# Transposing the next graph's x1 ahead of a graph's last product, in one stretch of a two-layer graph network

## The chip, the core and the metric

The kernel runs on one core of a Trainium2 chip. The core has five engines that run side by side, each with its own queue of instructions: TensorE (PE, matrix products; its weight loads are listed as PEld), VectorE (DVE), ScalarE (ACT), GpSimd (POOL) and SyncE (SP, which here only issues transfers). TensorE writes its results into banks of PSUM; everything else lives in SBUF or in DRAM. The metric is the device time of one execution in microseconds (us), the median of several.

## The reference

64 graphs of 256 nodes with 256 features go through two layers. Layer 0 is a normalised graph convolution, layer 1 a block made of a convolution along the nodes, an attention product and a gated unit. Cut to what is computed:

```python
# layer 0
deg = adj.sum(-1); d = where(deg != 0, deg, 1) ** -0.5
a_plus = d[:, :, None] * adj * d[:, None, :] + max(alpha, 1e-10) * eye(N)
x = layernorm(x + (a_plus @ x) @ W.T + b)              # called x1 in the kernel
# layer 1
h = relu(bn1(conv1(x.T)))                              # 1x1 convolution
x_conv = relu(bn2(conv2(h)) + x.T).T                   # 17 taps along the nodes
s = x @ w_se.T + b_se
A = exp(-dist(s, s)) * adj
x_nmp = A @ relu(x @ w_msg.T + b_msg)
x = layernorm(x + gru(concat(x_conv, x_nmp), x))       # gates r, z and candidate n
```

## The kernel before

The 17-tap convolution is done in the frequency domain. Sixteen graphs (Q) make a group, and there are four groups (NQ). For each graph `layer1` puts a small Fourier transform of h into a tile V; when a group is complete, `products` multiplies V with the transformed taps (matrices u, streamed from DRAM by SP), one step of 12 after another, and the inverse transform (`real_transform`, `complex_begin`, `complex_end`), which is vector work on VectorE, writes the convolution's result to DRAM. `gates` then runs the gated unit of each graph.

The work is written as generators that are woven into each other. `layer0` has three pieces, `layer1` seven. `graphs` runs `layer1` of graph g piece by piece, with pieces of `layer0(g + 2)` after pieces 1, 4 and 5, and of another stage (`others`) after pieces 0 and 5. The pieces of `layer1` are: (0) four transposes of x1 into a PSUM bank p_x1T and a copy on ScalarE into the first half of the tile xn (lines 413 to 420); (1) p_conv1, which reads that half, with VectorE adding the bias into h (line 431) and a relu on ScalarE (line 432); (2) p_msg; (3) p_dft, the Fourier transform of h (line 463), copied into V; (4) p_rows, with the copies dist_l on ScalarE and dist_r on VectorE; (5) p_dist (line 487), two Exp on ScalarE, and the product with the adjacency on VectorE (aT, line 489); (6) p_nmp (line 494), the graph's last product, copied into the second half of xn (line 498), which is then stored to DRAM (line 499). `layer0(g)` ends with p_out (line 398), VectorE's line 403 and a layernorm, whose power runs on GpSimd (line 314) and whose last step on ScalarE (line 324); that makes x1, two of which exist at a time. Its first piece transposes the adjacency (p_adjT, line 367, copied by line 368) and scales x (line 380).

The first sixteen graphs run while the weights are set up. Then the main loop goes over the groups q. While the products of group q run, the graphs of group q + 1 begin: the first AHEAD of them (12 for q = 0, 6 later) write their transforms into a second tile V2. With q = 0 no gates are due yet, so `others` is empty: three pieces of the graphs 16 to 27 are run after each of the 12 steps of products, and the rest is run by `paced`, which hands out pieces of `complex_end` on VectorE behind marked instructions of the graphs, 1.2 pieces for each mark. Then four copies on ScalarE (line 1031) bring V2 into V, the memory of V2 is given to the tiles of the gates, and the last four graphs (28 to 31) run with the first gates of group 0 as `others`. The gates' first pieces load xc_g (line 742) and the inputs (lines 746, 748), add x1 into xc_g by a transfer that GpSimd issues (line 753), transpose it (p_xcT, line 764), and form sums on GpSimd (lines 775 to 780).

Inside each engine the order isn't the order in which the program is written: a planner goes over all instructions, takes the written order as their priority, and gives each engine the instruction that its own estimate has ready. `issue_after` ties an instruction to a place behind another one. PSUM banks of `layer0` and `layer1` come from one ring of four (`bank`), in the order in which they are asked for.

Of the kernel before, what the change touches and what calls it, by code (L numbers as in the profile page):

```python
# [9 lines left out]
F32 = mybir.dt.float32  # L10
# [4 lines left out]
P = 128  # L15
# [11 lines left out]
def kernel(  # L27
# [27 lines left out]
    nc = tc.nc  # L55
    B, N, D = x.shape
# [4 lines left out]
    DCH = D // P  # L61
# [14 lines left out]
    work = ctx.enter_context(tc.tile_pool(name="work", bufs=2))  # L76
# [3 lines left out]
    def bank(name):  # L80
        return ps.tile([P, 512], F32, tag="bank", name=name)
# [7 lines left out]
    def mark(op):  # L89
        marks.append(op.ins)  # L90
# [238 lines left out]
    xc_d = [dram.tile([Q, N, D], F32, name=f"xc_d{q}") for q in range(NQ)]  # L329
    x1_d = [dram.tile([Q, N, D], F32, name=f"x1_d{q}") for q in range(NQ)]  # L330
    xn_d = [dram.tile([P, 2 * DCH, N], F32, name=f"xn_d{g}") for g in range(B)]
    ADJT, X1, X_SCALED, DIAGONAL = {}, {}, {}, {}


# [73 lines left out]
        nc.scalar.dma_start(x1_d[g // Q][g % Q].rearrange("(c p) d -> p c d", p=P), x1)  # L408
        yield

    def layer1(g, V, place):

        x1, adjT = X1.pop(g), ADJT.pop(g)
        xn = work.tile([P, 2 * DCH, N], F32, name="xn")
        x1T = xn[:, :DCH]
        p = bank("p_x1T").rearrange("p (k n) -> p k n", k=DCH)
        for k in range(DCH):
            for c in range(NCH):
                nc.tensor.transpose(p[:, k, c * P : (c + 1) * P], x1[:, c, k * P : (k + 1) * P], ident)
        nc.scalar.copy(x1T, p)  # L420

        yield

        h = work.tile([P, NCH, D + NSE], F32, name="h", bufs=1)
        for c in range(NCH):
            p = bank("p_conv1")[:, : D + NSE]
            for k in range(DCH):
                nc.tensor.matmul(  # L428
                    p, x1T[:, k, c * P : (c + 1) * P], wc1[:, k, :], start=k == 0, stop=k == DCH - 1
                )  # L430
            mark(nc.vector.tensor_tensor(h[:, c, :], p, bc1, op=ALU.add))
        nc.scalar.activation(h[:, :, :D], h[:, :, :D], AF.Relu)  # L432

        s3 = h[:, :, D:]
        cols = scols.rearrange("p c (q r) -> p c q r", r=32)
        nc.vector.tensor_copy(cols[:, :, :, :NSE], s3.unsqueeze(2).to_broadcast([P, NCH, 4, NSE]))
        sq3 = small.tile([P, NCH, NSE], F32, name="sq3")
        nc.vector.scalar_tensor_tensor(sq3, s3, -1.0, s3, op0=ALU.mult, op1=ALU.mult)
        nsq = small.tile([P, NCH], F32, name="nsq")
        nc.vector.tensor_reduce(nsq, sq3, AX.X, ALU.add)  # L440
        nc.vector.tensor_scalar(
            cols[:, :, 2:4, NSE], nsq.unsqueeze(2).to_broadcast([P, NCH, 2]), 0.5, None, op0=ALU.mult
        )
        yield
        msg = work.tile([P, NCH, D], F32, name="msg", bufs=1)
        p = bank("p_msg").rearrange("p (c d) -> p c d", c=NCH)
        for c in range(NCH):
            for k in range(DCH):
                nc.tensor.matmul(  # L449
                    p[:, c, :], x1T[:, k, c * P : (c + 1) * P], wmsg[:, k, :], start=k == 0, stop=k == DCH - 1  # L450
                )
        mark(nc.vector.tensor_tensor(msg, p, bmsg_t.unsqueeze(1).to_broadcast([P, NCH, D]), op=ALU.add))  # L452
        nc.scalar.activation(msg, msg, AF.Relu)
        yield


        mid = GT // 2
        for k in range(DCH):
            p = bank("p_dft")

            for c, t0, t1 in ((0, 0, mid + 1), (1, mid - 1, GT)):
                first = t0 + 1 - c * mid
                nc.tensor.matmul(  # L463
                    p[:, t0 * FL : t1 * FL], h[:, c, k * P : (k + 1) * P],
                    fwd[:, first : first + t1 - t0, :].rearrange("p t f -> p (t f)"),
                    start=c == 0, stop=True, skip_group_check=c == 1,
                )
            nc.scalar.copy(
                V[:, :, k, place * GT : (place + 1) * GT],
                p[:, : GT * FL].rearrange("p (t f) -> p f t", f=FL),  # L470
            )

        yield
        p = bank("p_rows")
        for c in range(NCH):
            nc.tensor.transpose(p[:, c * P : (c + 1) * P], scols[:, c, :], ident)
        dl = work.tile([64, N], F32, name="dist_l", bufs=1)
        nc.scalar.copy(dl, p[0:64, :N])
        dr = work.tile([64, N], F32, name="dist_r", bufs=1)
        nc.vector.tensor_copy(dr, p[64:P, :N])  # L480
        yield

        aT = work.tile([P, NCH, 2, P], F32, name="aT", bufs=1)
        for c in range(NCH):
            rows = slice(32 * c, 32 * c + 32)
            p = bank("p_dist")[:, :N]
            nc.tensor.matmul(p, dl[rows, c * P : (c + 1) * P], dr[rows, :], start=True, stop=True)
            nc.scalar.activation(aT[:, c].rearrange("p n q -> p (n q)"), p, AF.Exp, bias=nsq[:, c : c + 1], scale=2.0)  # L488
        mark(nc.vector.tensor_mul(aT, aT, adjT[:, :, 0:3:2, :]))  # L489
        yield  # L490
        p = bank("p_nmp").rearrange("p (k n) -> p k n", k=DCH)
        for k in range(DCH):
            for mc in range(NCH):
                nc.tensor.matmul(  # L494
                    p[:, k, :], msg[:, mc, k * P : (k + 1) * P], aT[:, mc].rearrange("p n q -> p (n q)"),
                    start=mc == 0, stop=mc == NCH - 1,
                )
        nc.scalar.copy(xn[:, DCH:], p)
        nc.scalar.dma_start(xn_d[g], xn)
        yield  # L500
# [5 lines left out]
    V, M = VM.rearrange("p f (k q) -> p f k q", k=DCH), VM  # L506
# [369 lines left out]
    def take(stage, n):  # L876

        for _ in range(n):
            if next(stage, "end") == "end":
                return  # L880
            yield
# [6 lines left out]
    def run(stage):  # L888
        for _ in stage:
            pass  # L890
# [18 lines left out]
    def graphs(first, part, V, others):  # L909


        for i in part:
            load(first + i + 3)
            given = {"layer0": layer0(first + i + 2) if first + i + 2 < B else iter(()), "other": others[i]}
            for piece, _ in enumerate(layer1(first + i, V, i)):
                yield
                for name in PLACES[piece]:
                    if next(given[name], "end") != "end":
                        yield
            yield from given["other"]  # L920
# [68 lines left out]
    def nothing():  # L989
        return iter(())  # L990
# [4 lines left out]
    scope, AHEAD, V2 = open_ahead(12)  # L995
    late = nothing()
    for q in range(NQ):
        first = (q + 1) * Q
        more = q + 1 < NQ
        end = complex_end(q)  # L1000
        if more:
            if q:
                others = [take(late, 3 if i % 3 == 0 else 2) for i in range(AHEAD)]
            else:
                others = [nothing() for _ in range(AHEAD)]
            begin = graphs(first, range(AHEAD), V2, others)
        sums(0)
        real = real_transform()
        for step in range(STEPS):
            if step < 4:  # L1010
                run(products(step))
            else:
                run(merge(products(step), take(real, 1)))
                run(complex_begin(step))
            if q:
                run(take(late, (0, 1, 1, 1, 1, 1, 2, 1, 2, 1, 2, 1)[step] if more else step % 2))
            else:
                run(take(begin, 3))
        run(real)
        if not q:  # L1020
            run(paced(begin, end, RATES[q]))
        elif more:
            run(paced(chain(merge(take(late, 20), take(begin, 6), 3), begin), end, RATES[q]))
        else:
            run(paced(late, end, RATES[q]))
            run(end)
        if more:
            run(late)
            run(end)
            for f in range(0, FL, 12):  # L1030
                nc.scalar.copy(V[:, f : f + 12, :, : AHEAD * GT], V2[:, f : f + 12])
            if q == 0:
                scope.close()
                gate = ctx.enter_context(tc.tile_pool(name="gate", bufs=2))
            early = gates(q, range(EARLY))
            others = [take(early, 5 if q == 0 else 2) for _ in range(Q)]
            run(graphs(first, range(AHEAD, Q), V, others))
            run(early)
            if q == 0:
                scope, AHEAD, V2 = open_ahead(6)  # L1040
                ctx.enter_context(scope)
            late = gates(q, range(EARLY, Q))
        else:
            run(gates(q, range(Q)))
# [53 lines left out]
```

## Time and profile before

| what | value |
|---|---|
| median of 3 runs | 2172.98 us (2172.46 to 2173.61) |
| the profiled execution | 2174.33 us, of which the span shown by the profile is 2172.5 us |
| instructions | 29034 |
| mean granted clock of TensorE | 0.989 of full speed |
| the stretch of graphs 16 to 27 | about 275 to 521 us from the span's start |
| of it, among the products of group 0 | 288 to 395 us |
| of it, with complex_end alone | 395 to 521 us |
| V2-to-V copies (line 1031) | 4 of about 2.1 us, at 515.17, 520.07 and two from 524.95 us |
| graphs 28 to 31 with the first gates | about 530 to 647 us |

The profile is of one execution. A timeline line gives the start in us, the busy time in us, the engine, the line of the kernel, the operation, what it writes and reads, and how many instructions were merged; in brackets stands how long the engine stood idle before it, and what ended that. A line of waits gives the engine and line that waited, for whom, the total in us, how often, and the longest. A matrix product in f32 shows as two records for each matmul of the program, so four matmuls are listed as 8; transposes are one record each. Busy times of consecutive products overlap a little, because the end of a product is modelled: the distance between the starts is the better measure of what one takes.

### The profile page before, as it was taken

The numbers are of one execution on the slowest core, as the hardware profiler recorded it, in microseconds if no ns is written. First come the engines' busy times: TensorE is split into PE (matmuls) and PEld (weight loads), VectorE is DVE, ScalarE is ACT, GpSimd is POOL, SyncE is SP. The second block draws the span as 40 slices with busy tenths as digits, with TensorE's granted clock in tenths as the row PEclk, the third lists the DMA queues.
The fourth block names the chain that finished last, engine by engine and source line by source line (L and its number), as shares of the span: only waits on it lengthen the run. The fifth ranks groups of instructions, "written<-read, shape, count | busy, mean of one in ns | idle before, by whom it ended". The sixth has DMA issues, their size and how long they took to land. (4 is left out here: it accounts for less than half of the span.)

```text
span 2172.5 us, 29034 instructions
## 1 busy us (share of the span) xinstructions
PE 2064.0 (95%) x9805; PEld 1748.4 (80%) x9805; DVE 1550.7 (71%) x3691; ACT 834.3 (38%) x1847; POOL 664.2 (31%) x640
## 2 busy tenths in 40 slices
PE   7999999887999999999999999899999998999998
PEld 5788788776788887788888888778888887788887
DVE  5555568785568798775556989775555889977776
ACT  4566643455331122455453122346543112222222
POOL 2444310211431233313222133323231123444442
PEclk9999999999999999999999999999999999999999
DMA  4765656434337644344335754334334844444442
GB/s 129 223 194 178 216 185 207 154 125 141 97 112 226 194 123 122 107 119 121 104 99 175 208 163 116 110 117 132 101 97 124 250 117 122 120 123 107 112 101 60
DMA packets 251182, 305.65 MB, mean 141 GB/s; under 512 B 18174, under 2 KB 229714, under 8 KB 251034
## 3 DMA queue, kind: packets, MB, share of 16 engines
q1 hardware_dynamic: 183530, 200.46, 30.4%
q10 hardware_dynamic: 44480, 67.39, 8.7%
q0 software_dynamic: 23024, 35.95, 8.6%
q8 instruction: 78, 1.28, 0.2%
q14 instruction: 70, 0.57, 0.1%
HBM read 200.62 MB, written 103.06 MB: 140 GB/s over the span
## 5 line engine op out<-in xcount | busy, mean ns | idle before, releaser
L833 PE MATMUL p_n<-wn,inputs 128*128 128x256 f32 x1536 | 355.9, 385 | 11.0 <-DVE first L809 10.6
L796 PE MATMUL p_rz<-wrz,sums 128*128 128x256 f32 x1536 | 350.9, 382 | 3.2 <-POOL sums L775 2.3
L833 PEld LDWEIGHTS p_n<-wn,inputs 128*128 128x128 f32 x1536 | 289.1, 192 | 58.1 <-DVE first L809 14.5
L796 PEld LDWEIGHTS p_rz<-wrz,sums 128*128 128x128 f32 x1536 | 290.7, 191 | 48.2 <-issue 5.9
L796 PE MATMUL p_rz<-wrz,inputs 128*128 128x256 f32 x1152 | 271.7, 379 | 0.4 <-ACT inputs L766 0.4
L314 POOL TENSOR_TENSOR ln_rs<-ln_rs,neg_half 128x2 f32<-128x2 f32 x129 | 101.2, 784 | 527.9 <-DVE ln_rs L313 417.4
L796 PEld LDWEIGHTS p_rz<-wrz,inputs 128*128 128x128 f32 x1152 | 217.5, 190 | 30.3 <-ACT inputs L766 1.0
L845 ACT ACTIVATE nn<-gn 128x256 f32<-128x256 f32 x128 | 53.2, 416 | 333.2 <-DVE gn L842 333.0
L518 PE MATMUL p_k<-u,VM 128*128 128x256 f32 x736 | 175.3, 380 | 4.1 <-DMA u<-ud 3.3
L775 POOL TENSOR_TENSOR sums<-inputs 128x384 f32<-128x384 f32 x64 | 67.8, 1059 | 335.1 <-ACT inputs L766 327.0
L358 POOL TENSOR_TENSOR dis<-deg,neg_half 128x2 f32<-128x2 f32 x64 | 46.5, 726 | 402.6 <-DVE deg L356 395.6
L324 ACT ACTIVATE x_g<-x_g,ln_mr,ln_rs 128x256 f32<-128x256 f32 x128 | 70.0, 593 | 245.6 <-DVE ln_mr L322 242.0
L518 PEld LDWEIGHTS p_k<-u,VM 128*128 128x128 f32 x736 | 138.1, 190 | 25.7 <-DMA u<-ud 3.4
L428 PE MATMUL p_conv<-wc,xn 128*128 128x259 f32 x512 | 128.8, 394 | 19.6 <-ACT xn L420 18.5
L388 PE MATMUL p_hT<-adjT,x 128*128 128x256 f32 x512 | 126.6, 390 | 9.5 <-DVE msg L452 4.9
L381 POOL TENSOR_TENSOR x_t<-x_t,b_t 128x512 f32<-128x512 f32 x64 | 86.4, 1350 | 146.7 <-ACT x L380 89.3
L463 PE MATMUL p_dft<-fwd,h 128*128 128x240 f32 x512 | 117.8, 373 | 13.9 <-ACT h L432 13.0
L428 PEld LDWEIGHTS p_conv<-wc,xn 128*128 128x128 f32 x512 | 97.1, 194 | 39.8 <-ACT xn L420 24.1
L489 DVE TENSOR_TENSOR aT<-aT,adjT 128x512 f32<-128x512 f32 x64 | 44.3, 692 | 115.3 <-ACT aT L488 115.3
L398 PE MATMUL p_out<-w,hT 128*128 128x256 f32 x512 | 123.9, 385 | 2.5 <-ACT hT L393 2.1
L449 PE MATMUL p_msg<-wmsg,xn 128*128 128x256 f32 x512 | 121.3, 379 | 0.0
L494 PE MATMUL p_nmp<-aT,msg 128*128 128x256 f32 x512 | 121.1, 379 | 0.2 <-DVE aT L489 0.2
(154 smaller groups left out, 3894.9 us busy)
## 6 DMA issues: line engine op xcount, KB each, us to landing
u<-ud SPq DMA_DIRECT2D x284, 256.0 KB
xn_d<-xn ACTq DMA_DIRECT2D x64, 512.0 KB
inputs<-xn_d SPq DMA_DIRECT2D x64, 512.0 KB
ud<-u_set POOLq DMA_DIRECT2D x39, 480.0 KB, 6.2
adj_t<-in_adj_dram SPq DMA_DIRECT2D x64, 256.0 KB
x_t<-in_x_dram SPq DMA_DIRECT2D x64, 256.0 KB
x_d<-x ACTq DMA_DIRECT2D x64, 256.0 KB
xc_d<-VM SPq DMA_DIRECT2D x64, 256.0 KB
```

What stands on the lines that cost most here:

```text
L314: nc.gpsimd.tensor_tensor(rs[:, : len(chunks)], rs[:, : len(chunks)], neg_half[:, : len(chunks)], op=ALU.pow)
L324: nc.scalar.activation(y[:, c, :], y[:, c, :], AF.Identity, bias=mr[:, c : c + 1], scale=rs[:, c : c + 1])
L381: nc.gpsimd.tensor_tensor(x_t, x_t, b0_t.unsqueeze(1).to_broadcast([P, NCH, D]), op=ALU.add)
L388: nc.tensor.matmul(p[:, k, :], x1[:, mc, k * P : (k + 1) * P], adjT[:, mc, 1 - mc : 3 - mc, :].rearrange("p n q -> p (n q)"), start=mc == ...
L398: nc.tensor.matmul(p[:, c, :], hT[:, k, c * P : (c + 1) * P], w0[:, k, :], start=k == 0, stop=k == DCH - 1)
L428: nc.tensor.matmul(p, x1T[:, k, c * P : (c + 1) * P], wc1[:, k, :], start=k == 0, stop=k == DCH - 1)
L449: nc.tensor.matmul(p[:, c, :], x1T[:, k, c * P : (c + 1) * P], wmsg[:, k, :], start=k == 0, stop=k == DCH - 1)
L463: nc.tensor.matmul(p[:, t0 * FL : t1 * FL], h[:, c, k * P : (k + 1) * P], fwd[:, first : first + t1 - t0, :].rearrange("p t f -> p (t f)") ...
L494: nc.tensor.matmul(p[:, k, :], msg[:, mc, k * P : (k + 1) * P], aT[:, mc].rearrange("p n q -> p (n q)"), start=mc == 0, stop=mc == NCH - 1,)
L518: nc.tensor.matmul(p[:, j * D : (j + 1) * D], v[:, k, :], u[:, k, :], start=k == 0, stop=k == DCH - 1)
L796: nc.tensor.matmul(p[:, j * D : (j + 1) * D], a[:, k], wrz[:, b, k], start=k == 0, stop=k == HALF - 1)
L833: nc.tensor.matmul(p[:, o * D : (o + 1) * D], lhsT, w, start=j == 0, stop=j == len(part) - 1)
```

## The change

The transposes of x1 and their copy are moved out of `layer1` into a function of their own, `x1_transposed(g)`, which keeps the tile in a table XN. `layer1(g)` calls it in piece 0 only if it has not been done. For the graphs in the set ALONE, piece 6 calls it for graph g + 1 just ahead of p_nmp. ALONE is filled in the main loop for q = 0 only, with graphs 16 to 27; so the transposes of graphs 17 to 28 move, and those of all other graphs stay where they were.

```diff
+    XN = {}
+    ALONE = set()
...
-    def layer1(g, V, place):
-
-        x1, adjT = X1.pop(g), ADJT.pop(g)
-        xn = work.tile([P, 2 * DCH, N], F32, name="xn")
-        x1T = xn[:, :DCH]
+    def x1_transposed(g):
+        x1 = X1.pop(g)
+        xn = XN[g] = work.tile([P, 2 * DCH, N], F32, name="xn")
         p = bank("p_x1T").rearrange("p (k n) -> p k n", k=DCH)
         for k in range(DCH):
             for c in range(NCH):
                 nc.tensor.transpose(p[:, k, c * P : (c + 1) * P], x1[:, c, k * P : (k + 1) * P], ident)
-        nc.scalar.copy(x1T, p)
-
+        nc.scalar.copy(xn[:, :DCH], p)
+
+    def layer1(g, V, place):
+
+        if g not in XN:
+            x1_transposed(g)
+        xn, adjT = XN.pop(g), ADJT.pop(g)
+        x1T = xn[:, :DCH]
         yield
...
         mark(nc.vector.tensor_mul(aT, aT, adjT[:, :, 0:3:2, :]))
         yield
+        if g in ALONE:
+            x1_transposed(g + 1)
         p = bank("p_nmp").rearrange("p (k n) -> p k n", k=DCH)
...
                 others = [nothing() for _ in range(AHEAD)]
+                ALONE.update(range(first, first + AHEAD))
             begin = graphs(first, range(AHEAD), V2, others)
```

## The prediction

> **What bounds the kernel now.** I began with the page: its busy table, then the costliest groups.
>
> ```profile
> PE 2064.0 (95%) x9805; PEld 1748.4 (80%) x9805; DVE 1550.7 (71%) x3691; ACT 834.3 (38%) x1847; POOL 664.2 (31%) x640
> ...
> L428 PE MATMUL p_conv<-wc,xn 128*128 128x259 f32 x512 | 128.8, 394 | 19.6 <-ACT xn L420 18.5
> ```
>
> TensorE (PE) is busy 95% of the span, so only the stretches where it stands still have anything to give. The wait that the change aims at is in the second line: p_conv, the first product of a graph, waits 18.5 us in all for the copy of the transposed x1 (line 420) on ScalarE (ACT). The same line asked by window puts most of it in the first group: 5.8 us in 8 waits between 395 and 522 us, and one of 7.63 us at 529.61.
>
> Then the busy times by stage. The change acts on graphs 17 to 28, which run from 288 to about 530 us: first among the first group's products, then with complex_end alone.
>
> ```profile
> core 0: us, PE busy (x) PEld busy (x) DVE busy (x) ACT busy (x) POOL busy (x), PEclk, DMA share, GB/s
> ...
> 288.30:395.00 106.70, 105.03 (x506) 90.07 (x506) 80.49 (x183) 37.42 (x80) 11.00 (x12) 1.00 0.71 224
> ...
> 402.04:521.38 119.34, 103.06 (x498) 81.56 (x497) 95.59 (x287) 67.77 (x154) 24.84 (x24) 1.00 0.38 122
> ...
> 521.38:535.10 13.72, 6.09 (x25) 4.93 (x24) 2.73 (x15) 8.89 (x11) 3.92 (x4) 0.75 0.61 198
> ```
>
> Among the products PE is idle 1.67 us of 106.70: full. From 402 to 521 us (eight graphs, some 15 us each) it is idle 16.3 us, and VectorE (DVE) is busy 95.59 us. From 521 to 535 us PE is busy less than half the time. Does PE or DVE set the pace in the second stretch? I asked what DVE waits for between 395 and 522 us; this is the whole answer.
>
> ```profile
> DVE aT L489 <- ACT aT L488: 16.4, 9, 2.8
> DVE ln_mr L322 <- POOL ln_rs L314: 4.9, 8, 0.7
> DVE dist_r L480 <- ACT dist_l L478: 3.0, 4, 1.0
> ```
>
> These three make 24.3 us, which is all of DVE's idle time (119.34 - 95.59 = 23.75). Each is a round trip of DVE's own results: dist_r to p_dist to Exp and back, the layernorm power on GpSimd (POOL), the rows. DVE never waits there for p_conv or p_msg. One boundary between two graphs shows why, in the timeline of all engines:
>
> ```profile
> 459.46 1.89 PE L494 MATMUL p_nmp<-aT,msg 128*128 128x256 f32 x8
> ...
> 461.19 0.60 PE L419 MATMUL p_x1T<-ident,x 128*128 128x128 f32 x4
> ...
> 461.87 0.59 ACT L420 COPY xn<-p_x1T 128x512 f32<-128x512 f32 x1
> ...
> 462.51 2.02 PE L428 MATMUL p_conv<-wc,xn 128*128 128x259 f32 x8 [0.73 <-ACT xn L420]
> ...
> 464.47 0.42 DVE L431 TENSOR_TENSOR h<-p_conv,bc 128x259 f32<-128x259 f32 x1
> ...
> 465.86 0.63 ACT L432 ACTIVATE h<-h 128x512 f32<-128x512 f32 x1 [0.27 <-DVE h L431]
> ...
> 466.55 1.89 PE L463 MATMUL p_dft<-fwd,h 128*128 128x240 f32 x8
> ```
>
> PE loses 0.73 us before p_conv. But half of p_conv is ready at about 463.5 us, and DVE takes it (line 431) only at 464.47, without an idle moment before: it was working on complex_end and the layernorm. The relu (line 432) ends at 466.49 and p_dft starts at 466.55. So p_dft is set by DVE and not by p_conv.
>
> Last, the timeline at the end of the stretch, between graphs 27 and 28:
>
> ```profile
> 520.07 2.10 ACT L1031 COPY VM<-V 128x2304 f32<-128x2304 f32 x1
> ...
> 521.38 0.60 PE L419 MATMUL p_x1T<-ident,x 128*128 128x128 f32 x4
> ...
> 524.95 4.12 ACT L1031 COPY VM<-V 128x2304 f32<-128x2304 f32 x2 [0.58 <-ACT x L324]
> 528.98 0.58 ACT L420 COPY xn<-p_x1T 128x512 f32<-128x512 f32 x1
> 529.10 0.38 SPq L742 DMA_DIRECT2D xc_g<-xc_d  x1
> ...
> 529.61 3.59 PE L428 MATMUL p_conv<-wc,xn 128*128 128x259 f32 x8 [7.63 <-ACT xn L420]
> ...
> 534.15 0.63 ACT L432 ACTIVATE h<-h 128x512 f32<-128x512 f32 x1
> ```
>
> The copy of x1T stands behind the V2-to-V copies (line 1031) on ACT; PE waits 7.63 us. When those copies end the next pool's memory is free, and SyncE's queue (SP) issues the first load of the gates, xc_g, at 529.10.
>
> **What the Trainium skill says.** "TensorE: Matmul & The Clock Gate", in its table and in Part 1 under "Architectural detail", has ACT, DVE and POOL as strict FIFOs. The trace agrees: line 420 waits 7 us behind copies it doesn't need. The same page, Part 1 ("The HAM clock gate"), gives PE half its clock after about 3.4 us idle. Here p_conv after the 7.63 us takes 3.42 us to the next product (529.61 to 533.03) where it takes 1.75 otherwise (355.31 to 357.06): 1.67 us lost.
>
> **The change part by part.** For graphs 17 to 28 four transposes and one copy move ahead of p_nmp of the graph before. Nothing is added, and no DMA moves. On PE they pass 8 matmuls; on ACT the copy passes the copy of p_nmp (line 498, 0.59 us) and the issue of xn_d's store (0.33 us). SP's and POOL's queues are passed by nothing. xn has two buffers: the one now taken a product earlier was stored at the end of the graph two before, some 15 us ago, so it costs nothing. p_conv's second half now takes the bank of p_out, which DVE empties (line 403) at 476.45 in the boundary at 476, against a need at about 477.4: nothing, with 0.9 us of cover. p_nmp comes 0.43 us later (292.65 to 293.08 is what four transposes take), and only its copy and store wait for it: nothing.
>
> *Graphs 17 to 19, among the products.* PE has no gap there but 0.16 us before one p_conv. I take -0.1 us; bounds 0 and -0.2.
>
> *Graphs 20 to 27.* Eight gaps of 0.73 us go, 5.8 us of PE idle time. What is late next is p_dft, which waits for the relu. Its time hangs on DVE, whose order I expect unchanged: what stands ahead of line 431 was traced before it. The slack left at p_dft is 0.17 us at 451.93, 0.4 at 510.95 and below 0.1 at most of the others, and later waits (p_hT for DVE, p_dist for dist_r) take that back. I take -0.3 us; bounds 0 and -5.8.
>
> *Graph 28.* p_out starts at 517.82 and takes 1.83; x1T at 519.65 takes 0.43; p_nmp 1.73, to 521.81. The copy of x1T then goes on ACT at the latest where line 498 went, 522.07: before line 324 ACT stands idle for 0.62 us, as long as one such copy, so the later V copies are not held up. p_conv starts 0.64 after (as at 461.87 to 462.51), 522.7; p_conv, p_adjT and p_msg (1.75 + 0.43 + 1.73 = 3.91) end at 526.6. Then p_dft waits for the relu, which I place right behind the V copies, as the transposed copy was: these end at 529.07, the relu at 529.7, p_dft starts at 529.8 instead of 535.20: 5.4 us earlier. If lines 380 and 368 (0.91 + 0.59) go first, 3.9. PE's new idle time is 3.2 us, so the 1.67 us of half clock may be lost again: 3.7 or 2.2. Then a cap: after p_nmp of graph 28 comes p_xcT of the first gate, at 543.16 without a wait. It needs the residual added into xc_g, issued on POOL at 532.12 and landing 8.1 us later, 540.2. That chain begins with the V copies and doesn't move. So no more than 2.9 us can be had, unless the load of adj_t (line 99, behind p_adjT and so earlier now) frees the DMA queues and it lands 0.9 earlier (3.8). A second half-clock spell while PE waits for the landing could take 1.7 back (1.2 left). I take -2.9; bounds -1.2 and -3.8. Behind p_xcT the next loads wait for its buffer, so they move with it, and from 550 us PE has little slack: the gain stays.
>
> The sum: -0.1 - 0.3 - 2.9 = -3.3 us on the profiled execution, 2174.33 (span 2172.5), which is 1.35 above the median 2172.98; off the median that is 2169.7 us.
>
> **The rivals.**
> A, the forecast, 0.45: 2169.7, by itself 2166.5 to 2172 (its bounds -1.2 to -3.8 and a part of the gaps).
> B, the gaps are paid in full, 0.27: all instructions are ordered by a planner, and with p_conv earlier in its plan, h may be put ahead of complex_end's work on DVE, which has 20% idle. Then -5.8 - 2.9 = -8.7, 2164.3. For it: DVE isn't full. Against it: DVE's idle time is all round trips of its own.
> C, it doesn't do what it says, 0.13: the copy of x1T is placed behind the V copies again, or the half clock takes the boundary's gain: 0 to -1, 2172.5.
> D, slower, 0.15: the copies of line 1031 give way. If x1T's copy and line 498 push the second one behind (2.1), and the relu, lines 368 and 380 (2.13 with their waits for PE of about 1) stand ahead of the last two, the copies end at about 534.3 instead of 529.07. xc_g then lands at 545.4, and with the half clock p_xcT's work runs as if begun at 547: +4 to +5, 2177.5. It decides from the point where the copies end later than 543.16 - 11.1 = 532.0. Against it: these copies come before graph 28's work in the program.
>
> **How the numbers follow.** About 0.2% (4.3 us) is what a measurement of this kernel can tell from no change. A lies mostly inside (0.32 of its 0.45); its other 0.13 and B's 0.27 make 0.40 for faster. C's 0.13 and A's 0.32 make 0.45 for the same; D is the 0.15 for slower. The range, 2163 to 2176, takes in B and the small end of D; about 0.2 is left out.
>
> **What would show it.** p_conv without a wait at the eight boundaries, but the graphs' period unchanged and longer waits before p_dft; at graph 28 p_conv near 522.7, the V copies still ending near 529, p_dft near 530, p_xcT of the first gate near 540.3. A stretch from 402 to 521 us shorter by several us would make B right; V copies that end after 532, D.

## The result, and the profile after

The changed kernel takes 2166.76 us (median of 10 executions, 2164.28 to 2169.92) against 2173.27 us for the kernel before in the same measurement: a ratio of 0.9974, with a 95% interval of 0.9966 to 0.9983. By the ratio that is 5.7 us less, between 3.7 and 7.4; the medians themselves lie 6.5 us apart. Where a gain in us stands beside a ratio below, it is taken from the ratio. The span of the profiled execution went from 2172.5 to 2165.1 us.

The page of the changed kernel comes first. Its lines are numbered a little differently: p_conv is line 434 now, h is 437, the relu 438, p_dft 469, p_nmp 502, the copy of p_nmp 506, the V copies 1040, the load of xc_g 750, p_xcT 772.

```profile
PE 2063.7 (95%) x9805; PEld 1749.6 (81%) x9805; DVE 1546.6 (71%) x3691; ACT 833.8 (39%) x1847; POOL 665.5 (31%) x640
...
L469 PE MATMUL p_dft<-fwd,h 128*128 128x240 f32 x512 | 120.2, 379 | 20.7 <-ACT h L438 19.7
...
L434 PE MATMUL p_conv<-wc,xn 128*128 128x259 f32 x512 | 126.2, 388 | 6.8 <-ACT xn L420 5.6
```

The page before has this line for p_dft:

```profile
L463 PE MATMUL p_dft<-fwd,h 128*128 128x240 f32 x512 | 117.8, 373 | 13.9 <-ACT h L432 13.0
```

The work is the same. TensorE's wait before p_conv fell from 19.6 to 6.8 us, but that before p_dft, for the relu of h, rose from 13.9 to 20.7 us. The waits of TensorE in the stretch of graphs 20 to 27 show the exchange. Before (395 to 522 us; who waited for whom, total, times, longest):

```profile
PE p_conv L428 <- ACT xn L420: 5.8, 8, 0.7
PE p_dist L487 <- DVE dist_r L480: 3.5, 5, 1.0
PE p_hT L388 <- DVE adjT L370: 2.3, 2, 1.5
PE p_hT L388 <- DVE msg L452: 1.9, 2, 1.1
PE p_out L398 <- ACT hT L393: 1.3, 1, 1.3
PE p_dft L463 <- ACT h L432: 1.2, 1, 1.2
...
```

After (392 to 518 us):

```profile
PE p_hT L390 <- DVE adjT L372: 7.7, 7, 2.1
PE p_dft L469 <- ACT h L438: 4.9, 6, 2.2
PE p_dist L493 <- DVE dist_r L486: 1.3, 2, 1.0
...
```

The eight waits before p_conv are gone, 5.8 us. In their place p_dft waits 3.7 us more for the relu, and p_hT 5.4 us more for the diagonal that VectorE adds to the adjacency (adjT), while some waits for msg, dist_r and hT are gone too. All of TensorE's waits in the two windows, those not shown too, are 16.7 us before and 14.7 after. One graph in TensorE's timeline, the one that answers to the boundary at 461 us of before:

```profile
458.05 0.60 PE L419 MATMUL p_x1T<-ident,x 128*128 128x128 f32 x4
458.49 1.89 PE L502 MATMUL p_nmp<-aT,msg 128*128 128x256 f32 x8
460.21 1.92 PE L434 MATMUL p_conv<-wc,xn 128*128 128x259 f32 x8
...
465.03 1.89 PE L469 MATMUL p_dft<-fwd,h 128*128 128x240 f32 x8 [0.73 <-ACT h L438]
...
468.67 1.97 PE L390 MATMUL p_hT<-adjT,x 128*128 128x256 f32 x8 [1.54 <-DVE adjT L372]
```

p_conv follows p_nmp without a gap, and the 0.73 us turn up two products later. The period of this graph, from p_out to p_out, is 15.09 us; it was 15.01.

The end of the stretch, graphs 27 and 28, in the timeline of all engines:

```profile
516.43 2.10 ACT L1040 COPY VM<-V 128x2304 f32<-128x2304 f32 x1
...
518.43 0.57 ACT L420 COPY xn<-p_x1T 128x512 f32<-128x512 f32 x1
519.06 2.02 PE L434 MATMUL p_conv<-wc,xn 128*128 128x259 f32 x8 [0.72 <-ACT xn L420]
...
521.78 4.12 ACT L1040 COPY VM<-V 128x2304 f32<-128x2304 f32 x2 [0.58 <-ACT xn L506]
...
525.81 0.63 ACT L438 ACTIVATE h<-h 128x512 f32<-128x512 f32 x1
525.93 0.37 SPq L750 DMA_DIRECT2D xc_g<-xc_d  x1
...
526.49 3.45 PE L469 MATMUL p_dft<-fwd,h 128*128 128x240 f32 x8 [3.24 <-ACT h L438]
```

And TensorE's timeline a little later:

```profile
534.51 1.89 PE L502 MATMUL p_nmp<-aT,msg 128*128 128x256 f32 x8
537.60 0.66 PE L772 MATMUL p_xcT<-ident,xc_g 128*128 128x128 f32 x4 [1.20 <-DMA xc_g<-x_d]
```

The copy of x1T stands ahead of the last V copies now, and p_conv starts 4.88 us after p_out of graph 27 instead of 11.79. TensorE then waits for the relu, which is behind the V copies, and p_xcT waits for the residual's transfer, which it did not before.

To see what belongs to the program, I divide every profile into three parts by the starts of TensorE's instructions. p_out is counted by the graph whose layer 1 is running, as in the prediction. The two kernels were each profiled a second time:

| profile | first product of the group to p_out of graph 19 | to p_out of graph 27 | to the next group's first product |
|---|---|---|---|
| before | 110.15 | 119.34 | 129.81 |
| before, again | 110.16 | 119.32 | 129.75 |
| the change | 109.07 | 118.18 | 126.37 |
| the change, again | 109.07 | 118.17 | 126.51 |

The sum is 5.5 to 5.7 us less (1.1 + 1.2 + 3.2 to 3.4), which agrees with the 5.7 us of the timing. What lies ahead of the group's first product differs between executions without a cause in the program: 285.15 to 288.33 us among the profiles whose instructions are the same up to there. The 1.4 us by which that part is shorter in the first profile of the change is such a difference.

### The profile page after: what moved, and what is told of

The parts are those of the page before. It is cut to its first block, busy times and chain, and to the rows that moved or that the text cites. A ratio compares the mean times of both kernels' runs of the same rounds, so it can differ in the third digit from the quotient of the medians.

```text
span 2165.1 us, 29037 instructions
## 1 busy us (share of the span) xinstructions
PE 2063.7 (95%) x9805; PEld 1749.6 (81%) x9805; DVE 1546.6 (71%) x3691; ACT 833.8 (39%) x1847; POOL 665.5 (31%) x640
## 5 line engine op out<-in xcount | busy, mean ns | idle before, releaser
L469 PE MATMUL p_dft<-fwd,h 128*128 128x240 f32 x512 | 120.2, 379 | 20.7 <-ACT h L438 19.7
L390 PE MATMUL p_hT<-adjT,x 128*128 128x256 f32 x512 | 126.7, 390 | 12.8 <-DVE adjT L372 7.7
L469 PEld LDWEIGHTS p_dft<-fwd,h 128*128 128x128 f32 x512 | 95.8, 192 | 41.2 <-ACT h L438 34.5
```

The lines of the kernel that those rows point to most:

```text
L390: nc.tensor.matmul(p[:, k, :], x1[:, mc, k * P : (k + 1) * P], adjT[:, mc, 1 - mc : 3 - mc, :].rearrange("p n q -> p (n q)"), start=mc == ...
L469: nc.tensor.matmul(p[:, t0 * FL : t1 * FL], h[:, c, k * P : (k + 1) * P], fwd[:, first : first + t1 - t0, :].rearrange("p t f -> p (t f)") ...
```

## The experiments

**Only graph 28, and all but graph 28.** The move is split in two. The first run fills the set with graph 27 alone, so that only the transposes of graph 28 move:

```diff
-                ALONE.update(range(first, first + AHEAD))
+                ALONE.add(first + AHEAD - 1)
```

> Only the transposes of graph 28 move (those of graphs 17 to 27 stay). If the gain sits at the boundary of graphs 27 and 28, as I hold: 3 to 5 us faster than before, half or more of what the whole change gives (6.5), with p_conv of graph 28 some 7 us earlier and p_xcT of the first gate bound by the landing of its residual. If the eight gaps of 0.73 us pay (rival): no more than 2 us faster.

The second leaves that one out:

```diff
-                ALONE.update(range(first, first + AHEAD))
+                ALONE.update(range(first, first + AHEAD - 1))
```

> The transposes of graphs 17 to 27 move, those of graph 28 stay. If VectorE sets the pace from 395 to 521 us: 1 to 2.5 us faster than before (products some 1, paced stretch some 1), with waits before p_dft and p_hT in the place of the eight waits before p_conv. If the gaps pay: 5 us or more faster, and each graph's period 0.7 us shorter.

Measured: 0.9987 (0.9981 to 0.9994) for graph 28 alone, 2.8 us less, and 0.9988 (0.9982 to 0.9995) for the others, 2.6 us less. Both are at the edge of what was expected, the first just below 3 us and the second just above 2.5. By these timings about half of the gain is one boundary of twelve, though with intervals of 1.3 to 4.1 and 1.1 to 3.9 us the halves are not known well. The profile of the second tells why the other eleven give no more. Its parts are 109.07, 119.93 and 129.75 us: the first is that of the change, the third that of before, and the middle one is longer than before although eight gaps of 0.73 us were taken out. TensorE's timeline in it:

```profile
494.65 2.98 PE L390 MATMUL p_hT<-adjT,x 128*128 128x256 f32 x8 [2.08 <-DVE adjT L372]
497.56 1.22 PE L493 MATMUL p_dist<-dist_r,dist_l 32*128 32x256 f32 x4
498.72 3.74 PE L400 MATMUL p_out<-w,hT 128*128 128x256 f32 x8
```

and its busy times by window, with the granted clock third from the end:

```profile
482.00:492.00 10.00, 9.83 (x52) 8.22 (x49) 8.14 (x25) 5.35 (x13) 0.81 (x1) 1.00 0.38 131
...
495.50:500.00 4.50, 4.50 (x13) 2.76 (x12) 0.73 (x2) 1.60 (x4) 0.79 (x1) 0.50 0.01 4
```

After a wait of 2.08 us TensorE ran at half its clock: p_out took 3.57 us from start to start instead of 1.83. The profile of the change has such a spell at another place, at graph 20:

```profile
404.00:409.20 5.20, 3.02 (x12) 2.53 (x12) 5.20 (x20) 3.41 (x7) 1.35 (x2) 0.81 0.34 116
409.20:412.00 2.80, 2.80 (x11) 2.12 (x12) 0.52 (x2) 0.93 (x4) 1.22 (x1) 0.75 0.30 99
```

There the period of the graph is 16.45 us; without the spell, in the second run, it is 15.08, as before. From p_out of graph 19 to the sixth p_out after it, where the second run has no spell, it takes 87.55 us against 87.75 of before: six gaps, 4.4 us in all, gave 0.2. In the run with graph 28 alone the first two parts are those of before (110.15 and 119.34) and the last is 128.22, which is 1.6 us less than before. Its timeline shows the two limits that the prediction named:

```profile
528.03 2.57 PE L469 MATMUL p_dft<-fwd,h 128*128 128x240 f32 x8 [3.29 <-ACT h L438]
...
538.31 0.66 PE L772 MATMUL p_xcT<-ident,xc_g 128*128 128x128 f32 x4 [0.37 <-DMA xc_g<-x_d]
```

The parts of these two profiles explain less than the timings: 1.6 of 2.8 us and 0.6 of 2.6. Each holds half-clock time that other executions need not have: with graph 28 alone p_out of graph 27 takes 2.84 us to the next start instead of 1.83, and in the second run the spell above costs some 3 us (119.93 us against 116.89 in the run with all groups moved, below, which has no spell there).

**A light VectorE.** If VectorE is what keeps the gaps from paying, they must pay where it has little to do. In both kernels complex_end of the first group was reduced to its stores:

```diff
     def complex_end(q):
 
+        if q == 0:
+            for i, n in enumerate((0, 8, 4, 12, 2, 10, 6, 14, 1, 9, 5, 13, 3, 11, 7, 15)):
+                yield
+                yield
+                low = CR + i
+                nc.sync.dma_start(
+                    xc_d[q].rearrange("g (t a b) d -> (g t) a b d", a=2, b=16)[:, :, n, :], M[:, low : low + 17 : 16, :]
+                )
+                yield
+            return
         yield from four(CR, CI)
```

> Leaves out complex_end's vector arithmetic for the first group (its 16 stores stay), without the change: the stretch of graphs 20 to 27 with VectorE far from full. Both theories: the stretch gets shorter than 119 us; the wait of 0.73 us before p_conv stays at every boundary.

> The same left out (complex_end's vector arithmetic for the first group), with the change. If VectorE is what kept the eight gaps from paying: each graph's period from 20 to 27 is 0.6 to 0.75 us shorter than in the run without the change, some 5 to 6 us over the stretch. If something else eats the gap (ScalarE, the order of PE): less than 0.3 us a graph.

Measured: 2160.66 us without the change and 2149.42 with it, four executions each. The change is worth 11.2 us here by the medians (12.6 by the ratios), about twice what it gives in the kernel as it is (6.5 and 5.7). TensorE's waits from 395 to 500 us, without the change:

```profile
PE p_conv L428 <- ACT xn L420: 5.8, 8, 0.7
PE p_dist L487 <- DVE dist_r L480: 1.0, 1, 1.0
```

and with it:

```profile
PE p_hT L390 <- DVE adjT L372: 1.4, 7, 0.2
PE p_out L400 <- ACT hT L395: 0.3, 1, 0.3
```

The period of most graphs is 13.65 us without the change, and 12.7 to 12.8 with it, 0.9 shorter, a little more than the 0.73 us of the gap and than the 0.6 to 0.75 expected. The three parts tell where the larger gain comes from: the first is 1.1 us shorter and the last 3.2, as in the kernel as it is, but the eight graphs take 102.45 us instead of 109.85, which is 7.4 less instead of 1.2. What was taken away is work on VectorE: in these eight graphs it is busy 95.3 us before and 54.3 in the light kernel without the change, while ScalarE stays at 66.7 and 66.3 (GpSimd has 24.8 and 21.2). So the load of VectorE is what swallows the gaps. The load of ScalarE and the order on TensorE are the same in the light kernels, and there the gaps pay.

**All groups.** The condition becomes true for every graph but the last:

```diff
-        if g in ALONE:
+        if g + 1 < B:
```

> All graphs but the first have their x1 transposed ahead of the last product of the graph before, in every group. If only the end of the first group's stretch holds a gain: within 2 us of the whole change. If the same move costs where gates are woven in: slower than the whole change by 2 us or more; if gaps pay anywhere: faster by 2 us or more.

Measured: 1.005 (1.0038 to 1.0062), slower by 10.9 us. TensorE's waits from 20 to 285 us, where the weights are set up beside the graphs, begin with this line; before, p_dft waited there once, for 2.5 us, and p_conv 6 times, for 4.3 us in all:

```profile
PE p_dft L469 <- ACT h L438: 13.8, 12, 1.9
```

This is the same exchange at a worse rate: the wait moves from p_conv to p_dft and grows. From 640 to 1670 us the waits before p_dft are 18.0 us instead of 7.8. The loss lies outside the stretch of the change. From the group's first product to the next group's this run takes 349.17 us, 10.1 less than before; the part ahead of it takes 293.95 us (288.33 at most in the other profiles), and the part behind it 1535.2 (1525.8 at most). Why the relu comes so much later there was not followed up.

**V copies on two engines.** At graph 28 VectorE stands idle while ScalarE copies V2 into V:

```diff
             for f in range(0, FL, 12):
-                nc.scalar.copy(V[:, f : f + 12, :, : AHEAD * GT], V2[:, f : f + 12])
+                copy = nc.vector.tensor_copy if q == 0 and f % 24 else nc.scalar.copy
+                copy(V[:, f : f + 12, :, : AHEAD * GT], V2[:, f : f + 12])
```

> The change, and two of the four V2-to-V copies of the first group on VectorE, which stands idle there. If the new limit at graph 28 is the V copies on ScalarE (relu behind them, and xc_g's load behind the memory that they free): the copies end about 2 us earlier, p_dft of graph 28 and p_xcT follow, and the time is 1 to 2.5 us below that of the change. If the limit is the landing of complex_end's last stores, or PE: the same as the change within 0.7 us.

Measured: 0.9971 (0.9958 to 0.9985), no different from the change. The copies did end earlier, 7.3 us after p_out of graph 27 instead of 11.7, and p_dft started after 9.3 us instead of 12.3. TensorE then stood still later (its timeline):

```profile
525.45 1.89 PE L469 MATMUL p_dft<-fwd,h 128*128 128x240 f32 x8 [1.21 <-ACT h L438]
...
531.20 1.20 PE L804 MATMUL p_rz<-wrz,inputs 128*128 128x256 f32 x4 [1.91 <-DMA inputs<-xn_d]
...
539.72 0.60 PE L772 MATMUL p_xcT<-ident,xc_g 128*128 128x128 f32 x4
```

The planner put four records of the first gate's p_rz ahead, where the gate's inputs had not landed, and after that wait the granted clock was 0.50 from 533.5 to 537.06 us. So p_xcT came 23.6 us after p_out of graph 27, as with the change (23.4). It no longer waited for the residual, which was issued at 527.62 and took 7.9 us to land: it stood behind p_nmp, which was late. The earlier copies did bring that transfer forward (11.5 us after p_out of graph 27 instead of 15.1), and a new order on TensorE and half-clock time took that back in this execution. The seven executions lie far apart (2161.9 to 2170.4 us), so whether other executions kept the gain is open.

**The move carried on to the end of the group.** The last four graphs, with the first gates woven in, were added (the edit moves the transposes of graphs 29 to 31; the expectation counts one graph too many):

```diff
-                ALONE.update(range(first, first + AHEAD))
+                ALONE.update(range(first, first + Q - 1))
```

> The change carried on through the last four graphs of the first group's stretch: the transposes of graphs 29 to 32 move too, where the first gates are woven in. In the run with every graph moved, the part from p_xcT of the first gate to the next group's products took 100.6 us instead of 103.0 to 104.5. If that belongs to these four graphs alone: 2 to 4 us faster than the change. If it came from the other groups' moves or from a missing half-clock spell: the same as the change within 1 us.

Measured: 0.9949 (0.9935 to 0.9962), 11.1 us less than before, 5.4 less than the change: the fastest of the kernels here that leave nothing out. Its parts are 109.07, 118.14 and 123.28 us; the last is 3.1 to 3.2 us shorter than with the change. TensorE's timeline there:

```profile
538.78 0.60 PE L772 MATMUL p_xcT<-ident,xc_g 128*128 128x128 f32 x4
539.22 1.92 PE L434 MATMUL p_conv<-wc,xn 128*128 128x259 f32 x8
540.98 1.02 PE L804 MATMUL p_rz<-wrz,inputs 128*128 128x256 f32 x4
544.63 5.45 PE L804 MATMUL p_rz<-wrz,sums 128*128 128x256 f32 x24 [2.63 <-POOL sums L783]
```

p_conv of graph 29 fills the time while the first gate's transposes are copied, and p_dft of graph 31, which waits 1.60 us with the change, follows p_msg at once. The other 2 us of the difference lie outside the three parts; the intervals are wide enough for that to be chance.

**Second profiles.** The two kernels as they are, for the table above:

> The change unaltered, for a second profile. If the parts of the gain belong to the program: 109.1 us from the first product of the group to p_out of graph 19, p_xcT of the first gate 23.4 us after p_out of graph 27, and waits before p_dft and p_hT. If the stretch from p_out of graph 19 to that of graph 27 (118.2) hangs on where half-clock spells fall: 116.5 to 120 us.

> The kernel before unaltered, for a second profile. If its parts belong to the program: 110.1, 119.3 and 25.3 us in the same three parts; what stands ahead of the group's first product (285 to 288 us) may differ by 3 us between executions.

The first two parts came out within 0.02 us of the first profiles in both kernels, and so did the spell at graph 20. The third figure did not repeat. From p_out of graph 27 to p_xcT it took 22.17 us (23.42 in the first profile), and 27.26 before (25.34). A half-clock spell that falls elsewhere roughly makes up for it each time: the 24 records of p_rz on the sums take 7.13 us in the second profile of the change and 5.45 in the first, and before they take 5.45 in the second and 7.13 in the first. So the third part as a whole stays within 0.15 us.

## Why the prediction was right, and where its sizes were off

The time is in the range, the direction is right and the rival on the slower side did not come: the V copies ended 11.7 us after p_out of graph 27, against 11.3 before. The gain of 5.7 us would be 2167.3 off the median of before, inside case A and near its fast end, where 3.3 us were taken as likeliest. The chances put a change too small to tell (0.45) a little ahead of a clear gain (0.40), and the gain was clear. The terms of the sum, one by one:

*The stretch of graphs 20 to 27, forecast -0.3, measured -1.16.* The main step, that p_dft is late next and that the load of VectorE keeps the gaps from paying, is shown by the exchange of waits and by the light VectorE. (The three waits of VectorE that it sums to 24.3 us are counted from 395 us. From 402 us, where the idle time of 23.75 us is counted, they are 23.0, and the reading stands.) Three things in it were different, and the small total is in part luck, because two of them work against each other.

First, the order was expected unchanged, and it changed. Here is ScalarE's timeline at graph 22, before and after:

```profile
434.82 1.09 ACT L324 ACTIVATE x<-x,ln_mr,ln_rs 128x256 f32<-128x256 f32 x2 [1.93 <-DVE ln_mr L322]
435.82 0.56 ACT L368 COPY adjT<-p_adjT 128x512 f32<-128x512 f32 x1
...
436.50 0.63 ACT L432 ACTIVATE h<-h 128x512 f32<-128x512 f32 x1
```

```profile
434.18 1.09 ACT L324 ACTIVATE x<-x,ln_mr,ln_rs 128x256 f32<-128x256 f32 x2 [0.36 <-DVE ln_mr L322]
435.19 0.63 ACT L438 ACTIVATE h<-h 128x512 f32<-128x512 f32 x1
...
435.72 0.58 ACT L370 COPY adjT<-p_adjT 128x512 f32<-128x512 f32 x1
```

The relu stood behind the copy of the adjacency in seven of the eight graphs; now it stands ahead of it in seven. On VectorE the two halves of h are added in one go in five graphs instead of two. This is what rival B asked for, h ahead of other work, and yet the gaps weren't paid: the diagonal of adjT, which needs that copy, is what p_hT now waits for. The relu isn't always set by VectorE either: in graphs 20, 21 and 24 it starts 0.6 to 0.8 us after h is complete, behind other work in ScalarE's own queue.

Second, in the first six graphs the gain was 0.2 us where no spell falls, as worked out, but in the last two it was 2.2: 29.35 us against 31.59. About half of this is one wait, that of p_out of graph 27 for hT, 1.33 us before and 0.20 after. Before, the first V copy (515.17 us, 2.1 long) stood ahead of the copy of hT on ScalarE; now it runs at 511.53, and the copy of hT follows at 513.55. Part of the rest may be an instruction of VectorE on four columns (line 441 of graph 26), which took 1.25 us in both profiles of before, beside an addition on GpSimd, and 0.17 with the change. How much of the 2.2 us the new order causes isn't shown.

Third, the half clock took 1.4 us back at graph 20. The prediction priced it for graph 28 alone. By its own logic the gaps of 0.73 us would gather into longer waits, and it did not ask what those do to the clock. Without a spell, in the run with all groups moved, the eight graphs take 116.89 us, 2.45 less than before.

*Graph 28, forecast -2.9, measured -3.2 to -3.4 for the last part.* The steps hold one by one, counted from p_out of graph 27: p_conv at 4.9 us (forecast 4.9), the V copies' end at 11.7 (11.3), p_dft at 12.3 (12.0) with the new idle time of 3.2 us and with the half clock (p_dft takes 3.24 us from start to start instead of 1.62), and p_xcT at 23.4 and 22.2 in the two profiles (22.5), on the landing of the residual (529.28 + 8.3 = 537.58, p_xcT 537.60; in the second profile 529.66 + 7.2 = 536.86, p_xcT 536.91). The size is less sure than it looks: p_xcT itself came 1.9 us earlier in the first pair of profiles and 5.1 in the second, and the spell on p_rz decides what is left of it. The run with graph 28 alone gave 2.8 us by itself.

*Graphs 17 to 19, forecast -0.1 with -0.2 as the bound, measured -1.08*, the same in every profile with the move. This is the term that was mis-sized most. The prediction counted idle time in brackets, 0.16 us, where the distance between starts was needed. Before, TensorE's timeline reads:

```profile
382.62 0.60 PE L419 MATMUL p_x1T<-ident,x 128*128 128x128 f32 x4
383.52 1.10 PE L518 MATMUL p_k<-u,VM 128*128 128x256 f32 x4 [0.30 <-DMA u<-ud]
384.79 2.02 PE L428 MATMUL p_conv<-wc,xn 128*128 128x259 f32 x8 [0.16 <-ACT xn L420]
386.64 0.60 PE L367 MATMUL p_adjT<-ident,adj_t 128*128 128x128 f32 x4
```

Four transposes take 0.44 us and four records of p_k 0.86, so the starts of p_k and p_conv are 0.46 and 0.41 late, and p_conv takes 1.85 us instead of 1.75: 0.97 us at this one boundary. The other 0.1 is at the boundary at 321 us. Now p_conv and p_adjT run there at once, and the next p_k comes 2.2 us later, without a wait for its u. The prediction said that there was no gap but the 0.16 us; the 0.30 for u, just ahead of it, stands in the same view.

*The gain stays*, it said, and it does: the three parts add up to the timing. Rival B's size, 8.7 us, did not come. What the forecast lacked were gains in places that it had called full or bound.

## What to carry to other kernels

A gap on the busiest engine is worth its length only if the next thing that this engine needs is not late as well: look for the instruction behind the gap that waits next, and ask whether the engine that it waits for was idle. A move like this one pays most where a long, unrelated job stands ahead of the small one on an in-order queue (here 2.8 us at one boundary, between 1.3 and 4.1), and it should be tried stretch by stretch: the same move in all groups made this kernel 10.9 us slower. A move of a few instructions can also change the order on other engines, so look at their queues again afterwards. Sum the distances between starts, not the bracketed idle times, when you price a stretch.

## What the hardware showed that I had not expected

Half-clock spells came after waits much shorter than the 3.4 us that the Trainium skill gives ("TensorE: Matmul & The Clock Gate", Part 1, "The HAM clock gate"): after 2.18 us at graph 20 with the change, and after 2.08 us in the run without graph 28. The same two waits had no spell the other way round: in the run without graph 28 TensorE waits 2.18 us at graph 20 (before p_dft at 404.93 us) and with the change 2.08 us (before p_hT at 497.26 us), and the granted clock behind them was 1.00. The page calls the window free-running, and the runs agree in that the idle length alone does not decide.

Fewer short waits and more long ones can cost clock, even with a smaller sum. In the two windows of waits above the kernel before has 16.7 us, none longer than 1.5 us, and the change 14.7, with one of 2.2 and one of 2.1 us. Of the six profiles with the full VectorE in which the transposes of these graphs had moved, five have a half-clock spell between p_out of graph 19 and that of graph 27; of the three without the move (before twice, graph 28 alone) none has. That the longer waits are the reason is likely, but it wasn't tested apart from the move.
